# A second, word-by-word load of layer 3's adjacency in place of its transposition on TensorE

## The chip, the cores and the metric

The kernel runs on one core of one Trainium2 chip. The metric is device time in microseconds, the time of that core from the first to the last instruction of one execution. Before the change three runs took 2528.9, 2530.66 and 2531.29 us; the median, 2530.66 us, is the time that the change is compared with.

A core has engines that run beside each other, each through its own list of instructions in a fixed order: PE (TensorE, matrix products and transpositions), DVE (VectorE), ACT (ScalarE), POOL (GpSimd) and SP (SyncE, used here for starting transfers alone). Transfers (DMA) are carried out by 16 DMA engines; an instruction on SP or on ACT starts one.

## The reference, cut to what matters

128 graphs of 64 nodes with 256 features each pass four layers. `adj` holds a 64x64 matrix of zeros and ones for each graph, in fp32; the inputs make it symmetric, but the kernel doesn't count on that.

```python
# layers 0 and 1: masked / weighted attention with 8 heads, layer 2: five GRU steps on the graph
# (most of the work), each with a layer norm and a relu ahead and a residual sum after.
# layer 3:
def _L3_gnn_ref(x, adj, theta, W_h, W_t, b_t):
    in_degrees = jnp.sum(jnp.abs(adj), axis=-1)
    norm = ((in_degrees + 1e-06) ** (-0.5))[..., None]
    f_hom = jnp.einsum('bnd,de->bne', x, theta) * norm
    f_hom = jnp.einsum('bnm,bmd->bnd', adj, f_hom) * norm      # <- needs adj turned, see below
    f_het = jnp.einsum('bnd,de->bne', x, W_h)
    gate = jax.nn.sigmoid(jnp.einsum('bnd,de->bne', x, W_t) + b_t)
    out = gate * f_hom + (1.0 - gate) * f_het
    return jax.nn.elu(out)
```

TensorE contracts over partitions, and its stationary operand stands with the contracted index on the partitions. For `adj @ f_hom` the contracted index is m, so the kernel needs adj with m on the partitions: adj turned. A load in the natural order has n there.

## The kernel before

Graphs go two by two: a pair fills the 128 partitions (two graphs of 64 nodes), and four pairs make a group, so there are 16 groups. Each group g passes a **front** (layers 0 and 1 and the preparation of what layers 2 and 3 need), an **entry** and five **GRU steps** (layer 2), and a **back** (layer 3). The fronts, steps and backs of neighbouring groups are interleaved: while group g is in its GRU steps, the front of a later one and the back of an earlier one fill the gaps.

The order of instructions on each engine is set when the program is built, by a list scheduler (`Plan`). Every operation is added with an engine, a guessed cost, a guessed latency to its users, what it reads and writes, and a **due time** (its key, in units of a group). The scheduler then steps through time: of the operations that are ready on an engine, it takes the one that is due first, but none that is due more than `AHEAD` later than the oldest one that still waits. Constants shift and stretch the due times of the parts:

```python
AFTER = {"PE": 210, "DVE": 125, "ACT": 145, "POOL": 90, "SP": 2500}   # guessed latencies, ns
GROUP = 157000                                                        # ns of a group, for due times
BESIDE, ALONE, TURNING, AHEAD = 0.45, 0.15, 0.25, 2.15
FRONT, FRONT_LAST, FRONT_SPAN = 0.1, 0.2, 0.95
BACK, BACK_LAST, BACK_SPAN = -0.1, 0.35, 0.65
...
# in Plan.run: users' due times are handed back to what they need
for op in reversed(self.ops):
    for u in op.users:
        op.key = min(op.key, u.key - (op.cost + self.delay(op, u)) / GROUP)
```

The values and buffers: `new(tag, shape, n)` takes one of n buffers of that name; `bank` is one of four PSUM banks shared by nearly everything that isn't a gate of the GRU. The part of the front that the change touches:

```python
def load_adj(i):                       # two groups' adjacency, natural order, on SP
    t = new("adjq", [P, n_adj, NODES], 2, f"adjq{i}")
    dma(256, lambda: nc.sync.dma_start(t.tile, adj_t[:, i * n_adj : (i + 1) * n_adj, :]), [], [t])

blk = filled("adjblk", [P, PAIRS, P], 0.0)          # once: zeros, 128 x (4 pairs x 128)

def front(g):
    adjq = adj_vals[g // ADJ_GROUPS][0]
    neg = ...                                        # mask for layer 0, from adjq
    for layer in range(2):
        for half in range(2):
            attend(layer, xt, half, ...)
    for gp in range(2):                              # the two graphs of a pair, on the diagonal
        s = slice(gp * NODES, (gp + 1) * NODES)
        pool(350, lambda s=s: nc.gpsimd.tensor_copy(blk[s, :, s], adjq[s, sel, :]), [adjq], [(blk, gp)])
    A = ...                                          # adj != 0, for layer 2 (DVE)
    deg = ...; norm = ...                            # sums over rows (DVE), power (POOL)
    adjT = new("adjT", [P, PAIRS, P], 4, f"adjT_{g}")
    ps = bank(f"adjT_{g}")
    def turn():                                      # 4 transpositions of 128 x 128
        for p in range(PAIRS):
            nc.tensor.transpose(ps[:, p * P : (p + 1) * P], blk[:, p, :], ident.tile)
    pe(437, turn, [blk, ident], [ps], holds=[adjT], mode=TURN)
    for p in range(PAIRS):                           # out of PSUM, times the norm of column m
        sca(act(P, 1), lambda p=p: nc.scalar.activation(
            adjT[:, p, :], ps[:, p * P : (p + 1) * P], AF.Identity, scale=norm[:, p : p + 1]),
            [ps, norm], [(adjT, p)])
    held[g] = xt, A, adjT, norm
```

`adjT` is used once, in the back, some 3.6 groups later (group 4: transposed at 422 us, used from 972 us):

```python
pe(mm(256), lambda p=p, f=f, ph=ph: nc.tensor.matmul(
    ph[:, :D], adjT[:, p, :], f(), start=True, stop=True), [adjT, (v, 0), (v, 1)], [ph], holds=[o])
```

Transfers are started by SP, but for one short block at the start, in which ACT starts six small ones (`fill_rows`: the rows of biases and the node mask). During the GRU steps SP loads 1344 KB of fused gate weights for each step (`gv`, two buffers) and, for the attention, seven blocks of 192 KB (`qw`, seven buffers).

Of the kernel before, what the change touches and what calls it, by code (L numbers as in the profile page):

```python
# [10 lines left out]
AF = mybir.ActivationFunctionType  # L11
# [12 lines left out]
P = 128  # L24
D = 256
NODES = 64
HEADS = 8
HD = 32
PAIRS = 4
# [20 lines left out]

WIDE, T64, T32, TURN = range(4)
CHANGE = ((0, 95, 95, 0), (250, 30, 135, 200), (237, 135, 30, 187), (0, 95, 95, 0))
BESIDE = 0.45
ALONE = 0.15
TURNING = 0.25
AHEAD = 2.15

FRONT = 0.1  # L60
FRONT_LAST = 0.2
FRONT_SPAN = 0.95
BACK = -0.1
BACK_LAST = 0.35
BACK_SPAN = 0.65
STEP = 0.0
STEP_LAST = -0.1
STEP_SPAN = 0.5
LOCK = 0.3
BACK_END = 0.1  # L70
ENTRY = -0.05
FIRST = -1.2
FIRST_SPAN = 1.15
ORDER = (0, 0, 1, 0, 1, 0)
FUSE = -1.1
FUSE_SPAN = 0.25
# [53 lines left out]
class Plan:  # L130
# [63 lines left out]
    def shift(last, mode, small):  # L194

        if mode in (T64, T32):
            return -BESIDE if last in (T64, T32) else ALONE if small < 2 else 0.0
        return -TURNING if mode == TURN and last in (T64, T32) else 0.0

    def run(self):  # L200
# [12 lines left out]
        for _ in range(len(self.ops)):  # L213
            while due[0] in done:
                due.pop(0)
            best, horizon = None, due[0].key + AHEAD
            for eng, ops in ready.items():
# [54 lines left out]
def gnn_stack_kernel(ctx: ExitStack, tc: tile.TileContext, a: dict, out: bass.AP):  # L272
    nc = tc.nc
    x, adj, nodemask = a["x"], a["adj"], a["nodemask"]
    n_pairs = x.shape[0] // 2
    n_groups = n_pairs // PAIRS
    scale = 1.0 / math.sqrt(HD)

    x_t = x.rearrange("(t a) n d -> (a n) t d", a=2)
    out_t = out.rearrange("(t a) n d -> (a n) t d", a=2)  # L280
    adj_t = adj.rearrange("(t a) n k -> (a n) t k", a=2)

    work = ctx.enter_context(tc.tile_pool(name="work", bufs=1))
    dram = ctx.enter_context(tc.tile_pool(name="dram", bufs=1, space=bass.MemoryType.DRAM))
# [3 lines left out]
    plan = Plan()  # L288
    tags = {}

    def new(tag, shape, n, name=None):
        if tag not in tags:
            home = psum if tag in ("a", "g") else dram if tag in ("gates", "kept") else work
            tags[tag] = Slots(home, tag, n, tag in ("g", "ht", "agg", "Ta", "Th", "gv", "qw", "hTQ", "qk", "kexp", "v"))
        return Val(tags[tag], name or tag, shape)

    def bank(name):
        return new("a", [P, 512], 4, name)
# [4 lines left out]
    def pe(cost, fn, reads, writes, early=0.0, holds=(), mode=WIDE, leaves=None):  # L303
        plan.add("PE", cost, fn, reads, writes, early=early, holds=holds, mode=mode, leaves=leaves)

    def vec(cost, fn, reads, writes, early=0.0):
        plan.add("DVE", cost, fn, reads, writes, early=early)

    def vec2(cost, fn, reads, writes, early=0.0):

        plan.add("DVE", cost, fn, reads, writes, early=early, port=True)
# [4 lines left out]
    def pool(cost, fn, reads, writes, early=0.0, port=1):  # L316
        plan.add("POOL", cost, fn, reads, writes, early=early, port=port)

    def dma(kb, fn, reads, writes, n=1):
        plan.add("SP", max(450 * n, 60 + kb * 5), fn, reads, writes)  # L320
# [6 lines left out]
    def load_adj(i):  # L327
        t = new("adjq", [P, n_adj, NODES], 2, f"adjq{i}")
        dma(256, lambda: nc.sync.dma_start(t.tile, adj_t[:, i * n_adj : (i + 1) * n_adj, :]), [], [t])
        adj_vals[i] = [t, None]  # L330
# [16 lines left out]
    def filled(tag, shape, value, on_dve=False):  # L347
        t = new(tag, shape, 1)
        n = 1
        for s in shape[1:]:  # L350
            n *= s
        if on_dve:
            vec2(n * 0.55 + 75, lambda: nc.vector.memset(t.tile, value), [], [t])
        else:
            pool(n * 0.88 + 50, lambda: nc.gpsimd.memset(t.tile, value), [], [t])
        return t
# [13 lines left out]
    with plan.strand(-3.0, 0.1):  # L370
# [13 lines left out]
        ident = new("ident", [P, P], 1)  # L384
# [40 lines left out]
        for c, tag in enumerate(("ht", "agg")):  # L425
            t = new(tag, [P, 3 * D], 2 if tag == "ht" else 1, f"w_ih{c}")
# [45 lines left out]
    with plan.strand(-0.3, 0.1):  # L472

        b_rz = new("b_rz", [P, 4], 1)
        vec(160, lambda: nc.vector.tensor_add(b_rz.tile, cols[:, 4:8], cols[:, 10:14]), [cols], [b_rz])
        vec(160, lambda: nc.vector.tensor_scalar(b_rz.tile, b_rz.tile, 0.5, None, op0=ALU.mult),
            [b_rz], [b_rz])


        b_n = new("b_n", [P, 2], 1)  # L480
        vec(160, lambda: nc.vector.tensor_sub(b_n.tile, cols[:, 8:10], cols[:, 14:16]), [cols], [b_n])


        w3 = new("w3", [P, 3, 8, P], 1)

        def load_w3():
            for i, name in enumerate(("L3_gnn_theta", "L3_gnn_W_t", "L3_gnn_W_h")):
                nc.sync.dma_start(w3[:, i, :4, :].rearrange("p (c o) q -> p c (o q)", c=2),
                                  a[name].rearrange("(c p) o -> p c o", p=P))

        dma(768, load_w3, [], [w3], 3)
        b_t = load_row("L3_gnn_b_t")
        blk = filled("adjblk", [P, PAIRS, P], 0.0)


    def power(dst, src, at, eps, n, name):
# [649 lines left out]
    def front(g):  # L1146

        if g % ADJ_GROUPS == 0 and (g // ADJ_GROUPS + 1) * ADJ_GROUPS < n_groups:
            load_adj(g // ADJ_GROUPS + 1)
        xt = x_vals.pop(g)  # L1150
        adjq = adj_vals[g // ADJ_GROUPS][0]
        sel = slice((g % ADJ_GROUPS) * PAIRS, (g % ADJ_GROUPS + 1) * PAIRS)
        first = (g % ADJ_GROUPS) * PAIRS
        neg = new("neg", [P, PAIRS, NODES], 1, f"neg_{g}")
        vec2(200, lambda: nc.vector.tensor_scalar(
            neg.tile, adjq[:, sel, :], 0.0, NEG, op0=ALU.is_le, op1=ALU.mult), [adjq], [neg])
        for layer in range(2):
            if layer and not g % ADJ_GROUPS:
                log_adj(g // ADJ_GROUPS)
            ladj = adj_vals[g // ADJ_GROUPS][1]  # L1160
            for half in range(2):
                bias = ladj if layer else neg
                bias_at = (lambda p, t=ladj, n=first: t.tile.rearrange("p t k -> p (t k)")[:, (n + p) * NODES : (n + p + 2) * NODES]) if layer else (
                    lambda p, t=neg: t.tile.rearrange("p t k -> p (t k)")[:, p * NODES : (p + 2) * NODES])
                attend(layer, xt, half, bias, bias_at, f"{g}_{layer}_{half}", g < 2 - layer)
                if g and g + 1 < n_groups and layer and not half:
                    load_x(g + 1)
                yield
        flush(xt)
        for gp in range(2):  # L1170
            s = slice(gp * NODES, (gp + 1) * NODES)
            pool(350, lambda s=s: nc.gpsimd.tensor_copy(blk[s, :, s], adjq[s, sel, :]), [adjq], [(blk, gp)])

        A = new("A", [P, PAIRS, NODES], 3, f"A_{g}")
        vec2(250, lambda: nc.vector.tensor_scalar(A.tile, adjq[:, sel, :], 0.0, None, op0=ALU.not_equal),
             [adjq], [A])
        deg = new("deg", [P, PAIRS], 2, f"deg_{g}")
        vec(310, lambda: nc.vector.tensor_reduce(
            deg.tile, adjq[:, sel, :], axis=AX.X, op=ALU.add, apply_absolute_value=True), [adjq], [deg])
        norm = new("norm", [P, PAIRS], 5, f"norm_{g}")  # L1180
        power(norm, deg, lambda: deg.tile, 1e-6, PAIRS, f"deg_{g}")
        adjT = new("adjT", [P, PAIRS, P], 4, f"adjT_{g}")
        ps = bank(f"adjT_{g}")

        def turn():
            for p in range(PAIRS):
                nc.tensor.transpose(ps[:, p * P : (p + 1) * P], blk[:, p, :], ident.tile)

        pe(437, turn, [blk, ident], [ps], holds=[adjT], mode=TURN)

        for p in range(PAIRS):
            sca(act(P, 1), lambda p=p: nc.scalar.activation(
                adjT[:, p, :], ps[:, p * P : (p + 1) * P], AF.Identity, scale=norm[:, p : p + 1]),
                [ps, norm], [(adjT, p)])
        held[g] = xt, A, adjT, norm

    def entry(g, xt):
# [147 lines left out]
    parts = {g: front(g) for g in range(n_groups)}  # L1345
    with plan.strand(FIRST, FIRST_SPAN):
        for g in ORDER:
# [18 lines left out]
    for at, g, l in events:  # L1366
        last = g + 1 == n_groups
        if l < 0:
            with plan.strand(begin[g] - 1 + FRONT + (FRONT_LAST if last else 0), FRONT_SPAN):
                for _ in range(4 - taken[g]):  # L1370
# [7 lines left out]
        if l == 0:  # L1378
            xt, A, adjT, norm = held[g]
            with plan.strand(begin[g] + ENTRY, 0.1):  # L1380
                h, ht = entry(g, xt)
            held[g] = xt, h, adjT, norm
            chains[g] = gru(h, ht, A, str(g), last)
        with plan.strand(at + STEP + (STEP_LAST if last else 0), STEP_SPAN):
            next(chains[g])
        if l + 1 == LAYERS:
            with plan.strand(begin[g] + 2 + BACK + (BACK_LAST if g + 2 == n_groups else BACK_END if last else 0), BACK_SPAN):
                back(g, *held.pop(g))
# [34 lines left out]
```

## Time and profile before

| what | before |
|---|---|
| median of three runs | 2530.66 us |
| span of the profiled run | 2527.0 us |
| PE busy | 2498.2 us (99%) |
| DVE busy | 2031.1 us (80%) |
| ACT busy | 1394.3 us (55%) |
| POOL busy | 879.0 us (35%) |
| the main queue's packets, share of 16 DMA engines | 21.8% |
| chain that ended last, share of PE | 96% |

The page gives each engine's busy time as a share of the span, then the span in 40 slices with one digit of busy tenths each. The chain that ended last is followed back from the last instruction: at each step to what released it, or to the instruction before it on its engine. A list of groups shows, for each line and operation, the number of instructions, their busy time, the mean of one, and the idle time of the engine before them with what ended it. TensorE's work is pipelined: neighbouring records overlap, so the time that an operation takes from TensorE is read from the starts of neighbouring instructions and not from one record's duration. "PEld" is the loading of the stationary operand, which overlaps the products. An engine's name with a q (SPq, ACTq) stands for its queue: there the instructions that start transfers are shown, which don't count as busy.

### The profile page before, as it was taken

The numbers are of one execution on the slowest core, as the hardware profiler recorded it, in microseconds if no ns is written. First come the engines' busy times: TensorE is split into PE (matmuls) and PEld (weight loads), VectorE is DVE, ScalarE is ACT, GpSimd is POOL, SyncE is SP. The second block draws the span as 40 slices with busy tenths as digits, with TensorE's granted clock in tenths as the row PEclk, the third lists the DMA queues.
The fourth block names the chain that finished last, engine by engine and source line by source line (L and its number), as shares of the span: only waits on it lengthen the run. The fifth ranks groups of instructions, "written<-read, shape, count | busy, mean of one in ns | idle before, by whom it ended". The sixth has DMA issues, their size and how long they took to land.

```text
span 2527.0 us, 58120 instructions
## 1 busy us (share of the span) xinstructions
PE 2498.2 (99%) x23491; PEld 2147.7 (85%) x23491; DVE 2031.1 (80%) x4632; ACT 1394.3 (55%) x2806; POOL 879.0 (35%) x892
## 2 busy tenths in 40 slices
PE   8999999999999999999999999999999999999998
PEld 6788888888888888888888888888888888888885
DVE  6876788887878888788877978878788887878667
ACT  4456555555555555565555655556555555655454
POOL 5533323324333233333323333243332333333221
PEclk9999999999999999999999999999999999999999
DMA  5421222113121122221222121131311222211120
GB/s 181 168 85 64 72 70 79 54 62 105 49 96 67 45 93 71 79 71 65 66 68 101 50 83 56 61 101 49 101 64 50 82 71 79 71 49 67 49 71 18
DMA packets 78256, 188.47 MB, mean 75 GB/s; under 512 B 14802, under 2 KB 66852, under 8 KB 67108
## 3 DMA queue, kind: packets, MB, share of 16 engines
q1 hardware_dynamic: 77872, 184.71, 21.8%
q8 instruction: 186, 3.05, 0.5%
q14 instruction: 82, 0.67, 0.1%
q10 hardware_dynamic: 116, 0.04, 0.0%
HBM read 166.70 MB, written 18.02 MB: 73 GB/s over the span
## 4 chain that ended last, share of the span: by engine, by line
PE 96%; DVE 3%; ACT 1%; DMA 0%; issue 0%; POOL 0%; SPq 0%; DVEq 0%; ACTq 0%; POOLq 0%
PE gb L924 22%; PE gc L924 17%; PE nb L924 11%; PE nc L924 8%; PE qkvb L674 6%; PE qkvc L674 5%; PE y L810 4%; PE agg L964 3%; PE l3b L1246 3%; PE s L736 3%; PE l3c L1246 2%; PE lnT L514 2%; PE hT L514 2%; PE aT L778 2%; PE o L797 2%; PE hom L1313 1%
## 5 line engine op out<-in xcount | busy, mean ns | idle before, releaser
L1033 POOL TENSOR_TENSOR sn<-h,sn 128x512 f32<-128x512 f32 x158 | 208.8, 1325 | 449.4 <-ACT sn L1031 449.1
L500 POOL TENSOR_TENSOR rstd<-pw,few 128x2 f32<-128x2 f32 x128 | 102.1, 798 | 478.1 <-DVE pw L499 461.3
L772 POOL TENSOR_TENSOR e<-e,ssum 128x512 f32<-128x512 f32 x128 | 149.9, 1178 | 312.3 <-DVE ssum L771 284.7
L924 PE MATMUL gb<-Th,w_hh 128*128 128x256 f32 x960 | 248.3, 381 | 0.0
L924 PE MATMUL gb<-Ta,gv 128*128 128x256 f32 x960 | 246.4, 379 | 0.0
L893 POOL TENSOR_TENSOR Th<-h 128x256 f32<-128x256 f32 x160 | 129.0, 826 | 270.0 <-PE nb L924 190.6
L924 PEld LDWEIGHTS gb<-Th,w_hh 128*128 128x128 f32 x960 | 178.0, 190 | 28.7 <-POOL Th L893 0.4
L924 PEld LDWEIGHTS gb<-Ta,gv 128*128 128x128 f32 x960 | 180.0, 190 | 25.5
L1031 ACT ACTIVATE sn<-sn,b_n 128x512 f32<-128x512 f32 x158 | 114.2, 724 | 129.7 <-DVE sn L1029 128.2
L924 PE MATMUL gc<-h,w_hh 128*128 128x256 f32 x640 | 165.9, 382 | 0.1
L924 PE MATMUL gc<-agg,gv 128*128 128x256 f32 x640 | 165.5, 381 | 0.0
L1035 DVE SCALAR_TENSOR_TENSOR sn<-sg,sn 128x512 f32<-128x512 f32 x158 | 107.3, 686 | 54.8 <-POOL sn L1033 54.3
L1016 ACT ACTIVATE sg<-sg,b_rz 128x512 f32<-128x512 f32 x158 | 105.6, 715 | 79.6 <-DVE sg L996 79.6
L924 PE MATMUL nb<-Th,w_hh 128*128 128x256 f32 x480 | 144.3, 382 | 0.0
L924 PE MATMUL nb<-Ta,gv 128*128 128x256 f32 x480 | 143.0, 380 | 0.0
L893 POOL TENSOR_TENSOR Th<-h,Th 128x256 f32<-128x256 f32 x160 | 137.9, 862 | 10.2 <-DVE h L1037 4.5
L810 PE MATMUL y<-w_L_gnn_Wo,oT 128*128 128x256 f32 x512 | 138.6, 382 | 1.5 <-DVE oT L805 1.4
L1027 DVE SCALAR_TENSOR_TENSOR sn<-sg,sn 128x512 f32<-128x512 f32 x158 | 110.2, 699 | 32.9 <-ACT sn L1138 29.1
L924 PEld LDWEIGHTS gc<-agg,gv 128*128 128x128 f32 x640 | 118.7, 190 | 17.1 <-issue 2.5
L977 DVE TENSOR_TENSOR Ta<-agg 128x256 f32<-128x256 f32 x160 | 90.2, 577 | 52.3 <-PE nb L924 40.7
L924 PEld LDWEIGHTS gc<-h,w_hh 128*128 128x128 f32 x640 | 116.6, 190 | 15.8 <-ACT sg L1023 0.5
L988 ACT ACTIVATE p5g<-gc 128x512 f32<-128x512 f32 x79 | 46.9, 593 | 149.4 <-PE gc L924 149.4
(223 smaller groups left out, 6931.9 us busy)
## 6 DMA issues: line engine op xcount, KB each, us to landing
gv<-gates SPq DMA_DIRECT2D x80, 1344.0 KB, 6.0
qw<-kept SPq DMA_DIRECT2D x203, 192.0 KB, 2.5
x<-in_x_dram SPq DMA_DIRECT2D x32, 256.0 KB, 5.6
out_dram<-x SPq DMA_DIRECT2D x32, 256.0 KB, 2.3
gates<-gv SPq DMA_DIRECT2D x5, 1344.0 KB, 4.7
adjq<-in_adj_dram SPq DMA_DIRECT2D x8, 256.0 KB, 3.0
gw<-in_L_gnn_weight_dram SPq DMA_DIRECT2D x5, 256.0 KB, 5.2
kept<-s SPq DMA_DIRECT2D x8, 128.0 KB
```

What stands on the lines that cost most here:

```text
L500: pool(660 if n == 2 else 970, lambda: nc.gpsimd.tensor_tensor(dst.tile, s.tile, few[:, 1 : 1 + n], op=ALU.pow), [s, (few, 1)], [dst], port=2)
L674: nc.tensor.matmul(bk[:, j * P : (j + 1) * P], lhs, rhs, start=first and j == 0, stop=True, skip_group_check=True)
L772: pool(1000, lambda e8=e8, z=z: nc.gpsimd.tensor_tensor(e8(), e8(), z[:, :, None].to_broadcast(shape), op=ALU.mult), [e, z], [e])
L810: pe(mm(256), lambda i=i, c=c: nc.tensor.matmul(py[:, i * D : (i + 1) * D], oT[:, i, c, :], w_o[:, c, :], start=c == 0, stop=c == 1), [(oT ...
L893: pool(690, lambda: nc.gpsimd.tensor_tensor(T[:, i, :], x(), y(), op=ALU.subtract), reads, [(T, i)])
L924: nc.tensor.matmul(bank_[:, col * HALF : (col + 1) * HALF], at(g, n), rhs(), start=first and j == 0, stop=True, skip_group_check=True)
L1016: sca(act(TOK, 1.5), lambda k=k, col=col: nc.scalar.activation(g_v[:, :, k, :], g_v[:, :, k, :], AF.Tanh, bias=b_rz[:, col : col + 1], sca ...
L1027: vec2(dve(TOK), lambda: nc.vector.scalar_tensor_tensor(a_(), r(), 1.0, a_(), op0=ALU.add, op1=ALU.mult), [*ts[0], n_v], [n_v])
L1031: sca(act(TOK, 1.5), lambda: nc.scalar.activation(a_(), a_(), AF.Tanh, bias=b_n[:, oc : oc + 1]), [n_v, b_n], [n_v])
L1033: pool(1230, lambda: nc.gpsimd.tensor_tensor(b_(), hh(), a_(), op=ALU.subtract), [*hp, n_v], [n_v])
L1035: vec2(dve(TOK), lambda: nc.vector.scalar_tensor_tensor(b_(), z(), 1.0, b_(), op0=ALU.add, op1=ALU.mult), [*ts[1], n_v], [n_v])
L1246: pe(mm(384), lambda: nc.tensor.matmul(bk[:, : 3 * P], b(), w3[:, :, n, :], start=first, stop=True, skip_group_check=True), [w3, *reads], ...
```

## The change: a load turned by the access pattern

The adjacency is in DRAM already, so it can be read a second time in another order. The new view has the contracted index k on the partitions:

```diff
     adj_t = adj.rearrange("(t a) n k -> (a n) t k", a=2)
+    adj_turned = adj.rearrange("(t a) n k -> a k t n", a=2)
```

On partition k it steps through n, and two neighbouring n lie 64 words apart in DRAM: each word of four bytes is a piece of its own. The front of each group starts eight such transfers from ACT's queue (2 graphs of a pair x 4 pairs, 64 x 64 words each) into the diagonal blocks of `adjT`, which POOL clears first. ACT then multiplies by the norm in place, from SBUF and no longer out of PSUM.

```diff
 def front(g):
     ...
+        adjT = new("adjT", [P, PAIRS, P], 4, f"adjT_{g}")
+        pool(620, lambda: nc.gpsimd.memset(adjT.tile, 0.0), [], [adjT])
+
+        def load_turned():
+            for gp in range(2):
+                s = slice(gp * NODES, (gp + 1) * NODES)
+                for p in range(PAIRS):
+                    nc.scalar.dma_start(adjT[s, p, s], adj_turned[gp, :, g * PAIRS + p, :])
+
+        plan.add("ACT", 1000, load_turned, [], [adjT], lat=30000)
     ... (mask, attention of layers 0 and 1)
-        for gp in range(2):
-            s = slice(gp * NODES, (gp + 1) * NODES)
-            pool(350, lambda s=s: nc.gpsimd.tensor_copy(blk[s, :, s], adjq[s, sel, :]), [adjq], [(blk, gp)])
     ... (A, deg, norm)
-        adjT = new("adjT", [P, PAIRS, P], 4, f"adjT_{g}")
-        ps = bank(f"adjT_{g}")
-
-        def turn():
-            for p in range(PAIRS):
-                nc.tensor.transpose(ps[:, p * P : (p + 1) * P], blk[:, p, :], ident.tile)
-
-        pe(437, turn, [blk, ident], [ps], holds=[adjT], mode=TURN)
 
         for p in range(PAIRS):
             sca(act(P, 1), lambda p=p: nc.scalar.activation(
-                adjT[:, p, :], ps[:, p * P : (p + 1) * P], AF.Identity, scale=norm[:, p : p + 1]),
-                [ps, norm], [(adjT, p)])
+                adjT[:, p, :], adjT[:, p, :], AF.Copy, scale=norm[:, p : p + 1]),
+                [adjT, norm], [(adjT, p)])
```

The buffer of zeros, `adjblk`, goes, with its one memset. For the scheduler, the eight starts are one operation of ACT with a cost of 1000 ns, whose result is there 30000 ns later.

The due times are set anew with it, so the order of instructions on every engine changes somewhat:

```diff
-BESIDE = 0.45            +BESIDE = 0.25
-AHEAD = 2.15             +AHEAD = 2.1
-FRONT_LAST = 0.2         +FRONT_LAST = 0.15
-BACK_SPAN = 0.65         +BACK_SPAN = 0.6
-STEP_LAST = -0.1         +STEP_LAST = -0.15
-BACK_END = 0.1           +BACK_END = 0.05
-ENTRY = -0.05            +ENTRY = 0.15
-FIRST = -1.2             +FIRST = -1.4
-FIRST_SPAN = 1.15        +FIRST_SPAN = 1.55
```

The change is for TensorE: it takes the transpositions of the adjacency, their PSUM bank and POOL's copies out of the program, and gives the turning to the DMA engines.

More of the change, by code (lines that the diff above doesn't have):

```diff
@@ L52 @@
 CHANGE = ((0, 95, 95, 0), (250, 30, 135, 200), (237, 135, 30, 187), (0, 95, 95, 0))
-BESIDE = 0.45
+BESIDE = 0.25
 ALONE = 0.15
 TURNING = 0.25
-AHEAD = 2.15
+AHEAD = 2.1
 FRONT = 0.1
-FRONT_LAST = 0.2
+FRONT_LAST = 0.15
 FRONT_SPAN = 0.95
@@ L64 @@
 BACK_LAST = 0.35
-BACK_SPAN = 0.65
+BACK_SPAN = 0.6
 STEP = 0.0
-STEP_LAST = -0.1
+STEP_LAST = -0.15
 STEP_SPAN = 0.5
 LOCK = 0.3
[L70 to L73, printed above, removed]
+BACK_END = 0.05
+ENTRY = 0.15
+FIRST = -1.4
+FIRST_SPAN = 1.55
 ORDER = (0, 0, 1, 0, 1, 0)
@@ L492, in gnn_stack_kernel @@
         b_t = load_row("L3_gnn_b_t")
-        blk = filled("adjblk", [P, PAIRS, P], 0.0)
     def power(dst, src, at, eps, n, name):
```

## The prediction, made before the changed kernel was run

> **What bounds the kernel now.** I read the page's busy shares first, then the chain that ended last, and then the waits of TensorE.
>
> ```profile
> PE 2498.2 (99%) x23491; PEld 2147.7 (85%) x23491; DVE 2031.1 (80%) x4632; ACT 1394.3 (55%) x2806; POOL 879.0 (35%) x892
> ...
> PE 96%; DVE 3%; ACT 1%; DMA 0%; issue 0%; POOL 0%; SPq 0%; DVEq 0%; ACTq 0%; POOLq 0%
> ```
>
> PE is busy for 2498.2 of 2527.0 us, and 96% of the chain is PE. A busy share alone can mislead, so I asked who PE waits for, and for the busy time of the steady part (158 to 2212 us):
>
> ```profile
> PE pc L449 <- DMA w_v<-in_L_gnn_Wv_dram: 8.9, 1, 8.9
> PE y L810 <- DVE oT L805: 1.4, 1, 1.4
> PE f L1217 <- ACT hT L519: 1.4, 2, 1.1
> PE gb L924 <- ACT agg L970: 1.2, 2, 0.9
> ...
> 158.00:2212.00 2054.00, 2052.02 (x19675) 1782.95 (x19674) 1677.40 (x3855) 1160.04 (x2359) 710.89 (x704) 1.00 0.22 71
> ```
>
> The columns of the waits are total, times and longest in us. One wait of 8.9 us stands at the start, for the first data; no other is above 1.4 us in total. In the second view the first pair is length and PE busy: in 2054 us PE lacks 2 us. So the kernel is bound by PE's instruction stream: whatever leaves PE comes off the time, and whatever makes PE wait is added in full, as PE has no idle time in which to catch up.
>
> Now the part that the change removes. This is the view of the tile adjT, and one stretch of PE's timeline:
>
> ```profile
> L1187 PE MATMUL adjT<-ident,adjblk x64: 272/273/329, 36.5 to 2107.8; 128*128 128x128 f32 x64
> L1172 POOL COPY adjblk<-adjq x32: 391/487/631, 31.3 to 2011.3; 64x256 f32<-64x256 f32 x32
> L1192 ACT ACTIVATE adjT<-adjT,norm x64: 359/378/410, 50.4 to 2109.1; 128x128 f32<-128x128 f32 x64
> ...
> 1187.91 0.60 PE L1187 MATMUL adjT<-ident,adjblk 128*128 128x128 f32 x4
> 1188.35 1.03 PE L924 MATMUL gc<-Th,w_hh 128*128 128x256 f32 x4
> ```
>
> One record lasts 273 ns, but the four of a group start at 1187.91 and the next product at 1188.35: four transpositions take 0.44 us from PE, 0.11 us each.
>
> **What the Trainium skill says.** TensorE: Matmul & The Clock Gate, section Part 4: PE-mode transpose, gives some 275 ns for a 128x128 transposition in a kernel, in bf16. This trace's fp32 records agree (273 ns), but what one takes away in a stream is 0.11 us; the measured spacing decides. DMA: Bandwidth & Descriptors, section Rules for kernel authors, says that a strided last dimension is lowered to one descriptor for each element, and that a transposition by rearranged access pattern is 19 times slower than the chip's own DMA transposition. The kernel before has no such transfer, so its trace can't confirm that. The section Issuing engines are not separate DMA queues of that page says that transfers started from ACT and from SP run on the same 16 DMA engines and interleave. So ACT's queue brings no bandwidth of its own.
>
> **The change part by part.**
>
> *Off PE.* 16 groups x 0.44 us = **7.0 us**. This is on the path in full. The PSUM bank that it held is worth nothing visible, as PE waits for no bank.
>
> *POOL.* It loses 32 copies x 487 ns = 15.6 us and one memset; it gains 16 memsets of 128x512, for which the memset of adjblk has a duration (542 ns): 8.7 us. POOL is busy 35%: no effect.
>
> *ACT's 64 multiplications* stay (378 ns each, now from SBUF). No effect.
>
> *The DMA engines.* A group's eight transfers carry 8 x 4096 words; by the skill one descriptor each, so over 16 engines 2048 for each engine and group. What does a word cost? Two stretches give the time of a packet: between 1514 and 1516 us the adjacency is loaded in 1024 packets of 256 B, and from 10 to 15 us weights in packets of 1024 B.
>
> ```profile
> 1514.00:1515.00 1.00, 1.00 (x7) 0.87 (x6) 0.32 (x1) 0.89 (x2) 0.65 (x1) 1.00 0.90 207
> 1515.00:1516.00 1.00, 1.00 (x6) 0.90 (x5) 0.97 (x2) 0.19 (x1) 0.00 (x0) 1.00 0.25 55
> ...
> 10.00:15.00 5.00, 4.31 (x13) 3.47 (x13) 1.79 (x8) 0.60 (x1) 0.70 (x1) 1.00 1.07 357
> ```
>
> The last two columns are DMA share and GB/s. (0.90 + 0.25) us x 16 / 1024 = 18 ns for 256 B; 1.07 x 5 us x 16 / (1785 KB / 1 KB = 1743) = 49 ns for 1024 B. The straight line through both meets 4 B at about 8 ns. My estimate is 8 to 15 ns a word; the kernel's own guess (30 us for 2048) is the upper end. So a group's turned load keeps all 16 engines occupied for **16 to 30 us out of 153**, and the DMA share rises from 22% to 32 to 42%. In steady state this is hidden: the turned adjacency is needed 3.6 groups later (group 4: transposed at 422 us, used from 972 us), and the gate weights (6.0 us to land) have a whole GRU step, some 30 us, between the release of a buffer and its next use. Slowed twofold for 30 us they are still in time, mostly.
>
> *The start.* There it is not hidden so well. Up to 25 us the DMA share is about 1 (1.07 above, 1.09 from 20 to 25 us), and PE's first weights come in that stretch. adjT has four buffers and ACT is idle early, so the first turned loads go out in the first tens of us and share the engines with those weights. I expect a delay of **3 to 12 us**, of which I take 6.
>
> *Starting eight transfers on ACT.* This is the dear part. At the start of the kernel before, ACT starts the rows and the mask; this is its queue:
>
> ```profile
> 1.34 0.24 ACTq L395 DMA_DIRECT2D rows<-in_L_gnn_bk_dram  x1
> 1.61 0.27 ACTq L395 DMA_DIRECT2D rows<-in_L_gnn_b_ih_dram  x1
> 1.92 0.32 ACTq L395 DMA_DIRECT2D rows<-in_L_gnn_b_hh_dram  x1
> ...
> 3.51 0.60 ACTq L397 DMA_DIRECT2D rows<-in_nodemask_dram  x1
> ```
>
> A start takes 0.24 to 0.60 us, say 0.38: eight take 3.0 us in one piece, against 1.0 us in the plan. ACT's order is fixed, so all behind it comes up to 2 us late. Does PE feel it? One case: the second agg copy leaves ACT at 662.33 us and PE's product with it starts at 663.10, 0.8 us of slack. ACT stands idle for 45% of the span, but in short pieces: in the steady part I count 24 idle stretches of at least 2.6 us, under two for each group. I take half of the 2 us as lost, with a spread of 0 to 1.5 us for a group: 16 x 0.6 = **10 us**, from my choice of 0.6.
>
> Sum: -7.0 + 6 + 10 = +9 us. The new due times can take back some of it; such a retuning is worth a few us at most where PE already has 2 us of idle time in 2054. I take -3, so about +6: **2537 us**.
>
> **The rivals.**
>
> *A: PE's gain comes through whole.* If starts on ACT fall into its idle time and the startup keeps its pace, -7 us and perhaps a little more from the due times: 2518 to 2524 us. For it speaks that PE hardly ever waits in the kernel before, although the plan's costs are guesses: its slack absorbs errors of some tenths of a us. Against it speaks that 3 us isn't some tenths.
>
> *B: ACT is held at the starts.* If a start can't be handed over until the transfers ahead of it have made room, ACT stands for most of the 16 to 30 us of each group, and PE with it: 16 x 5 to 20 us, or 2600 to 2850 us. The queue of SP speaks for it a little: behind the large stores at the start, four starts together took 6.95 us and a single one of x 1.59 us:
>
> ```profile
> 71.66 6.95 SPq L565 DMA_DIRECT2D kept<-s  x4
> 78.65 1.59 SPq L343 DMA_DIRECT2D x<-in_x_dram  x1
> ```
>
> (the first with waits for data in it). Against it: behind loads alone, with 1 MB and more outstanding in the first 17 us, SP's starts kept to 0.37 to 0.65 us. But no transfer there had 256 pieces for each engine. I give a clear form of this a little over one in five.
>
> *C: the weights come late.* The words and the gate weights share the engines, and a gv or qw load that lands after its turn stops PE for some us in each group: 2540 to 2600 us. Against it: the slack above, some 30 us against a burst of 16 to 30.
>
> **Range and chances.** A alone gives the low end, 2516 with a little from the due times. My sum stands at 2537. B and C make the tail above; I put the high end at 2620. Two per cent are 50.6 us: faster by that much would need seven times what leaves PE, 0.01; slower, above 2581 us, is B or a strong C, 0.22; the rest, 0.77, is within.
>
> **What would show it.** (1) PE has 64 instructions less, and its busy time falls by 7 us. (2) The queue of ACT shows 128 starts: at 0.3 to 0.4 us each my lumps are right; at 1 us or more it is B. (3) The waits of PE show new entries with ACT as releaser, 0.3 to 1.5 us each, some 10 us in sum; if there are none, A. (4) PE busy in the first 160 us (146.9 before) is some us lower. (5) The DMA share in the steady part is 0.32 to 0.42; gv takes more than 6.0 us to land in the median of its slow loads, but no PE wait names gv or qw; if one does, C. The prediction fails if ACT's starts block it, or if the time of a word is far above 15 ns.

## The result and the profile after

The changed kernel takes **2864.18 us** in the median (four runs, 2863.6 to 2865.23) against 2529.96 us for the kernel before on the same chips: 1.132 times the time, 95% interval 1.130 to 1.134. The prediction was 2537 us with a range of 2516 to 2620 us. It was wrong, and by far.

The page of the changed kernel, the parts that answer to those shown of the kernel before (busy times, DMA queues, the chain that ended last):

```profile
PE 2534.1 (89%) x23427; PEld 2158.6 (75%) x23427; DVE 2030.9 (71%) x4632; ACT 1411.8 (49%) x2806; POOL 839.8 (29%) x875
...
q1 hardware_dynamic: 77872, 184.71, 19.5%
q10 hardware_dynamic: 526452, 2.15, 10.5%
...
PE 71%; ACTq 8%; DVE 5%; POOL 2%; issue 2%; ACT 1%; POOLq 0%; DVEq 0%
PE gb L924 18%; PE gc L924 12%; PE nb L924 9%; ACTq L1162 8%; PE nc L924 6%; PE qkvb L674 5%; PE qkvc L674 3%; PE y L810 3%; PE agg L964 2%; PE l3b L1246 2%; PE hT L514 2%; PE l3c L1246 2%; PE lnT L514 2%; PE aT L778 2%; PE o L797 1%
```

The chain points to the place: PE's share falls from 96% to 71%, and 8% of the span is `ACTq L1162`, the line that starts the turned loads. PE has its 64 instructions less. It is idle for 2861.8 - 2534.1 = 328 us, against 29 us before.

The waits of PE (total, times, longest in us), and the tile adjT (durations in ns, least/median/most):

```profile
PE nb L924 <- DVE sg L996: 203.1, 12, 17.5
PE q L629 <- ACT hT L519: 49.8, 1, 49.8
PE aT L778 <- POOL e L772: 21.3, 2, 20.5
...
L1162 ACTq DMA_DIRECT2D adjT<-in_adj_dram x128: 602/2354/5930, 5.1 to 2421.6; - x128
L1313 PE MATMUL hom<-F,adjT x128: 379/379/483, 442.0 to 2854.1; 128*128 128x256 f32 x128
```

A start on ACT takes 2.35 us in the median, where the prediction took 0.38. PE now has a pause of 17 us in each of 12 groups and one of 50 us at the start. The waits don't name ACT in the groups, and here one has to look further: PE waits for DVE's `sg`, but that stood behind something itself. This is one group in order of time, ACT first, then DVE, then PE:

```profile
1011.85 17.88 ACTq L1162 DMA_DIRECT2D adjT<-in_adj_dram  x8
1029.77 0.72 ACT L1332 ACTIVATE F<-F 128x256 f32<-128x256 f32 x2 [17.98 <-DMA adjT<-in_adj_dram]
...
1030.22 0.42 DVE L1334 SCALAR_TENSOR_TENSOR o<-o,F 128x256 f32<-128x256 f32 x1 [16.61 <-ACT F L1332]
1032.50 0.68 DVE L996 TENSOR_TENSOR sg<-gc,ug 128x512 f32<-128x512 f32 x1
...
1015.67 1.03 PE L810 MATMUL y<-w_L_gnn_Wo,oT 128*128 128x256 f32 x4
1033.23 1.22 PE L924 MATMUL nb<-h,w_hh 128*128 128x256 f32 x2 [16.54 <-DVE sg L996]
1034.25 1.91 PE L924 MATMUL gb<-Th,w_hh 128*128 128x256 f32 x4
1035.95 1.78 PE L924 MATMUL gb<-h,w_hh 128*128 128x256 f32 x4
```

From 1011.85 to 1029.73 us ACT does nothing but start eight transfers. DVE, whose order is fixed as well, soon waits 16.6 us for ACT's Exp on F, and its sg, for which PE's next product waits, stands behind that. PE stops some 5 us after ACT and begins again 3.5 us after it. The products that follow are slow as well: four products take 1.7 us from one start to the next, where 0.86 is usual. The same stretch in windows (length, busy of PE, PEld, DVE, ACT, POOL, then TensorE's granted clock, DMA share, GB/s):

```profile
1015.00:1020.00 5.00, 1.70 (x8) 1.14 (x6) 0.00 (x0) 0.00 (x0) 0.00 (x0) 1.00 0.95 7
1020.00:1025.00 5.00, 0.00 (x0) 0.00 (x0) 0.00 (x0) 0.00 (x0) 0.00 (x0) 0.54 0.94 7
1025.00:1030.00 5.00, 0.00 (x0) 0.00 (x0) 0.00 (x0) 0.23 (x1) 0.00 (x0) 0.50 0.89 6
1030.00:1035.00 5.00, 1.77 (x4) 1.49 (x5) 4.78 (x11) 1.83 (x4) 0.00 (x0) 0.50 0.69 59
1035.00:1040.00 5.00, 5.00 (x19) 4.07 (x18) 3.95 (x8) 1.53 (x3) 1.27 (x1) 0.75 0.38 105
1040.00:1045.00 5.00, 5.00 (x83) 4.26 (x82) 4.78 (x14) 3.90 (x9) 1.67 (x2) 1.00 0.00 0
```

While ACT is held, the DMA engines are 90 to 95% busy and move 6 to 7 GB/s: words of four bytes. And the clock granted to PE falls to a half during the pause and stays there for some us after it.

The 335 us by which the span grew come from two parts. This is the product that uses adjT in the kernel before:

```profile
L1313 PE MATMUL hom<-F,adjT x128: 379/379/483, 363.7 to 2519.3; 128*128 128x256 f32 x128
```

adjT is first used at 442.0 us in place of 363.7: **78 us at the start**. From then on the first use in one group and in the next lie (2183.0 - 442.0) / 10 = 174.1 us apart (groups 0 to 10), before (1891.7 - 512.5) / 9 = 153.2 (groups 1 to 10; the first interval is shorter there, 148.8 us): **20.9 us for each of 12 groups, 251 us**. Together 329; most of the rest is that first interval. At the start the queue of ACT shows this, sixteen starts in a row with the first activation behind them (it begins at 58.7 us, before at 10.2):

```profile
5.06 52.27 ACTq L1162 DMA_DIRECT2D adjT<-in_adj_dram  x16
57.36 1.28 ACT L519 ACT_TABLE_LOAD   x1 [57.36 <-DMA r_L_gnn_bo<-in_L_gnn_bo_dram]
```

### The profile page after: what moved, and what is told of

The parts are those of the page before. It is cut to its first block, busy times and chain, and to the rows that moved or that the text cites. A ratio compares the mean times of both kernels' runs of the same rounds, so it can differ in the third digit from the quotient of the medians.

```text
span 2861.8 us, 58190 instructions
## 1 busy us (share of the span) xinstructions
PE 2534.1 (89%) x23427; PEld 2158.6 (75%) x23427; DVE 2030.9 (71%) x4632; ACT 1411.8 (49%) x2806; POOL 839.8 (29%) x875
## 3 DMA queue, kind: packets, MB, share of 16 engines
q10 hardware_dynamic: 526452, 2.15, 10.5%
## 4 chain that ended last, share of the span: by engine, by line
PE 71%; ACTq 8%; DVE 5%; POOL 2%; issue 2%; ACT 1%; POOLq 0%; DVEq 0%
PE gb L924 18%; PE gc L924 12%; PE nb L924 9%; ACTq L1162 8%; PE nc L924 6%; PE qkvb L674 5%; PE qkvc L674 3%; PE y L810 3%; PE agg L964 2%; PE l3b L1246 2%; PE hT L514 2%; PE l3c L1246 2%; PE lnT L514 2%; PE aT L778 2%; PE o L797 1%
## 5 line engine op out<-in xcount | busy, mean ns | idle before, releaser
L924 PE MATMUL gb<-Th,w_hh 128*128 128x256 f32 x960 | 259.8, 395 | 10.6 <-POOL sn L1033 10.6
L924 PE MATMUL nb<-h,w_hh 128*128 128x256 f32 x160 | 55.4, 431 | 203.1 <-DVE sg L996 203.1
L772 POOL TENSOR_TENSOR e<-e,ssum 128x512 f32<-128x512 f32 x128 | 139.3, 1099 | 285.7 <-DVE ssum L771 140.9
L924 PEld LDWEIGHTS nb<-h,w_hh 128*128 128x128 f32 x160 | 29.7, 208 | 214.4 <-DVE sg L996 212.0
L1334 DVE SCALAR_TENSOR_TENSOR o<-o,F 128x256 f32<-128x256 f32 x64 | 26.7, 417 | 207.3 <-ACT F L1332 207.0
L1035 DVE SCALAR_TENSOR_TENSOR sn<-sg,sn 128x512 f32<-128x512 f32 x158 | 107.0, 683 | 77.8 <-POOL sn L1033 77.4
L1332 ACT ACTIVATE F<-F 128x256 f32<-128x256 f32 x64 | 25.2, 412 | 256.7 <-DMA adjT<-in_adj_dram 202.1
L893 POOL TENSOR_TENSOR Th<-h,Th 128x256 f32<-128x256 f32 x160 | 128.3, 802 | 7.6 <-DVE h L1037 4.5
```

Of the source, the lines that this page charges most:

```text
L772: pool(1000, lambda e8=e8, z=z: nc.gpsimd.tensor_tensor(e8(), e8(), z[:, :, None].to_broadcast(shape), op=ALU.mult), [e, z], [e])
L893: pool(690, lambda: nc.gpsimd.tensor_tensor(T[:, i, :], x(), y(), op=ALU.subtract), reads, [(T, i)])
L924: nc.tensor.matmul(bank_[:, col * HALF : (col + 1) * HALF], at(g, n), rhs(), start=first and j == 0, stop=True, skip_group_check=True)
L1035: vec2(dve(TOK), lambda: nc.vector.scalar_tensor_tensor(b_(), z(), 1.0, b_(), op0=ALU.add, op1=ALU.mult), [*ts[1], n_v], [n_v])
```

## The experiments

Theory 1 was that ACT is held at its starts because the words ahead of them have yet to be drained (rival B of the prediction). Its rivals were the number of starts, the load on the DMA engines as such, and the new due times. Unless it is said, an experiment has the new due times and is told against the changed kernel.

### The same eight starts with rows in place of words

```diff
-    adj_turned = adj.rearrange("(t a) n k -> a k t n", a=2)
+    adj_turned = adj.rearrange("(t a) n k -> a n t k", a=2)
```

The turning is left out. As adj is symmetric in these inputs, the sums stay the same.

> The same eight starts for each group on ACT, at the same places, but in natural order: 64 rows of 256 B in place of 4096 words each (the turning is left out; adj is symmetric in these inputs, so the sums are the same). Theory 1 (ACT is held because the words queue up): a start takes 0.3 to 0.6 us, eight 2.5 to 4 us; time 2525 to 2545 us. Rival (any eight starts in one piece on ACT, or the new due times, cost the time): 2780 us or more.

Measured: 2643.13 us, 1.045 times before (1.043 to 1.046). It lies between the two forecasts and meets neither. The tile adjT and one group:

```profile
L1162 ACTq DMA_DIRECT2D adjT<-in_adj_dram x128: 472/607/1805, 5.4 to 2201.2; - x128
...
903.27 5.00 ACTq L1162 DMA_DIRECT2D adjT<-in_adj_dram  x8
908.32 0.72 ACT L1332 ACTIVATE F<-F 128x256 f32<-128x256 f32 x2 [5.10 <-DMA adjT<-in_adj_dram]
911.78 0.75 PE L924 MATMUL nb<-h,w_hh 128*128 128x256 f32 x2 [3.59 <-DVE sg L996]
...
PE nb L924 <- DVE sg L996: 52.5, 12, 4.9
```

With rows a start takes 0.61 us in the median and ACT is held for 5 to 6 us, not for 18; so the words account for 221 of the 334 us. But eight starts in one piece cost 113 us even so: a group is 161.4 us long, 8.2 us more than before. A piece of 5 us on ACT stops PE for 3.6 us here (52.5 us in 12 such waits, 4.4 us each), and a slower clock follows it.

### Half of the words

```diff
-  nc.scalar.dma_start(adjT[s, p, s], adj_turned[gp, :, g * PAIRS + p, :])
+  nc.scalar.dma_start(adjT[s, p, s.start : s.start + 32], adj_turned[gp, :, g * PAIRS + p, :32])
```

Half of the turned adjacency is left out.

> The eight starts carry 32 columns each, half of the words (2048, 128 for each DMA engine); half of the turned adjacency is left out. Theory 1: ACT is held about half as long, 8 to 10 us a group in place of 18; time 2660 to 2720 us. If the limit is a number of words that may wait, two or three starts at the head of each eight are short (0.4 to 0.7 us); if it is one transfer at a time, the second already takes about 1.2 us. Rival (the number of starts counts): 2850 us.

Measured: 2751.67 us, a single run. Nearly halfway between rows and words, and above what theory 1 gave; that forecast did not have in it what eight starts in one piece cost even with rows, 113 us.

```profile
L1162 ACTq DMA_DIRECT2D adjT<-in_adj_dram x128: 602/1358/4257, 5.2 to 2311.0; - x128
961.51 10.37 ACTq L1162 DMA_DIRECT2D adjT<-in_adj_dram  x8
```

ACT is held for 10.4 us in that group. In the later groups, the first start of each eight takes 0.60 us and the second already 1.2 us or more (602 and 1209 ns in this group); with all words it is 0.60 and then 2.1 to 3.6 us. A packet of one word takes 9.1 ns: 10.5% of 2861.8 us on 16 engines, over 526452 packets. So 128 words for each engine are 1.2 us and 256 are 2.3 us, about what a start takes when another stands ahead of it. From ACT one such transfer is drained, it seems, before the next is handed over.

The times from start to landing, where the traces have them, fit this: in the median 2.1 us with rows, 4.4 with half of the words and 6.6 with all. What comes on top of the rows is about two drains, 2 x 1.2 and 2 x 2.3 us, one for the transfer ahead and one for the transfer itself. It also shows that the start isn't held until the transfer ahead has landed. Whether it is held until the last word has moved or only until the last word has been handed to the DMA engines, these runs don't separate.

### Eight starts apart from each other, on ACT

```diff
-        plan.add("ACT", 1000, load_turned, [], [adjT], lat=30000)
+        for i in range(2 * PAIRS):         # each at least 3.5 us after the one before
+            gp, p = i % 2, i // 2
+            s = slice(gp * NODES, (gp + 1) * NODES)
+            plan.add("ACT", 600, lambda s=s, gp=gp, p=p: nc.scalar.dma_start(
+                adjT[s, p, s], adj_turned[gp, :, g * PAIRS + p, :]),
+                [(adjT, ("w", i - 1))] if i else [], [(adjT, ("w", i))],
+                lat=3500 if i < 2 * PAIRS - 1 else 8000)
```

> All words, all eight starts on ACT, but as eight operations of their own that the scheduler puts at least 3.5 us apart, each planned with 0.6 us. Theory 1: each start then finds the one ahead of it drained (2.3 us) and takes 0.6 us; ACT is held 5 us a group in eight small pieces, PE loses 0 to 0.5 us for each; time 2525 to 2590 us. Rival (the words disturb by their load on the DMA engines, wherever their starts stand): 2780 us or more.

Measured: 2568.35 us, 1.016 (1.014 to 1.017). The same words on the same queue of the same engine, and 296 us of the 334 are gone:

```profile
L1161 ACTq DMA_DIRECT2D adjT<-in_adj_dram x128: 602/603/7181, 5.5 to 2153.1; - x128
L1313 PE MATMUL hom<-F,adjT x128: 379/379/483, 390.2 to 2552.9; 128*128 128x256 f32 x128
```

The median of a start is 0.60 us, as forecast, and a group is 153.5 us long, 0.3 more than before. From 539 to 2072 us PE is busy for 1532.97 of 1533 us, at a DMA share of 0.35. This rules out the load on the DMA engines as the main cause. What is left is the start of the kernel: adjT is first used at 390.2 us, 26 us later than before and 36 us later than in the run with the due times alone (below), which is the closer comparison; 38 us of time are left to explain. Starts there take up to 7.2 us, while the weights come (DMA share 1.00 in the first 160 us).

### The same on SP

`nc.sync` in place of `nc.scalar`, and "SP" in place of "ACT" in the plan.

> The same eight spaced starts on SP, which does nothing but start transfers. Theory 1: no compute engine is held; gate weights can come 2 to 5 us late, within their slack of some 30 us; time 2518 to 2540 us, near the 7 us that left PE. Rival (the words make gv and qw late): PE waits for gv or qw by several us a group, 2600 us or more.

Measured: 2548.44 us, 1.007 (1.006 to 1.009); above the forecast, far below the rival. The start is as fast as before (first use at 358.3 us); SP starts the first turned load at 18.6 us, behind those of weights, where ACT started it at 5.1. But a group takes 154.9 us, 1.7 us more than before and 1.2 more than with the due times alone (153.7). The waits of PE show most of that:

```profile
PE gb L924 <- POOL sn L1033: 9.7, 11, 0.9
...
PE qkvb L674 <- DMA qw<-kept: 3.1, 1, 3.1
```

The wait of 0.9 us for POOL's `sn` comes in 11 groups and not once in the run with the due times alone. Why `sn` comes late here is open.

### The due times alone

The kernel before with the nine new constants.

> The kernel before with the nine new due times alone; the transpositions on TensorE stay. Theory 1 (ACT held by the turned loads is the cost): the due times are a matter of a few us, 2520 to 2550 us. Rival (the due times, fitted to the plan and not to the chip, are a main part): 2580 us or more.

Measured: 2530.55 us, 0.9999 (0.999 to 1.0008). The due times neither cost nor bring anything that can be measured here.

```profile
L1313 PE MATMUL hom<-F,adjT x128: 379/379/483, 354.3 to 2517.3; 128*128 128x256 f32 x128
```

They do move its parts: adjT is first used 9 us sooner than before, and a group takes 153.7 us, 0.5 more. Set against this run, which has the changed kernel's due times and the turning of before, the start of the changed kernel costs 88 us and not 78, and a group 20.4 us and not 20.9.

### No turning at all: the bound of the gain

The due times of before; the second load is out, and POOL copies the natural blocks to adjT:

```diff
-  (memset of adjblk, copies to adjblk, four transpositions, activation out of PSUM)
+  pool(620, lambda: nc.gpsimd.memset(adjT.tile, 0.0), [], [adjT])
+  pool(350, lambda s=s: nc.gpsimd.tensor_copy(adjT[s, :, s], adjq[s, sel, :]), [adjq], [(adjT, ("b", gp))])
+  (activation in place, as in the changed kernel)
```

> Bound of the gain: no second load and no transposition, POOL copies the natural blocks straight into adjT, due times of before (the turning is left out; adj is symmetric in these inputs). What leaves PE is 16 x 0.44 us = 7.0 us: 2520 to 2526 us. Rival (the transpositions filled gaps that other work doesn't): 2528 us or more.

Measured: 2527.5 us, 0.999 (0.998 to 0.9999), between the two. Of 7.0 us, 2.4 arrive. A group is 153.4 us long, not 152.8 (153.2 less 0.44): with 0.44 us less to do, the scheduler finds another order, and in it other seams open. In eight groups there are 64 places before where PE goes from wide products to small ones (agg, s and o, in tiles of 64 or 32 rows), and 72 here. Such a seam takes 0.3 us from one start to the next, where 0.22 is usual between wide products, and the way back 0.17 us, where small products follow each other in 0.02. By these figures, 8 more seams with their ways back make about 0.2 us a group (an estimate); the rest of the 0.6 us is open.

### Spaced starts with the due times of before, on ACT and on SP

> The turned load in eight spaced starts on ACT, with the due times of before. If the new due times cost the 38 us that the spaced starts with the new times stood above before: about 2530 us. If it is the start of the kernel, where the words share the DMA engines and hold ACT while the weights come: 2545 to 2570 us, with PE some 25 us short of before in the first 160 us.

> The turned load in eight spaced starts on SP, with the due times of before. If the due times are to blame for the slower groups (154.9 us in place of 153.2), the group falls to about 152.7 us and the time to 2520 to 2528 us, faster than both kernels. If SP's held queue is (gate and attention weights some us late), the group stays at about 155 us and the time at 2540 to 2555 us.

Measured: 2586.53 us on ACT (1.023, 1.021 to 1.025), above the range given, and 2550.08 us on SP (1.008, 1.007 to 1.010). Neither becomes faster than the kernel before. In both a group takes 154.8 us in the median. As it is the same on ACT and on SP, a held SP is hardly the reason here. In both there are 88 seams in eight groups, 24 more than before, by the figures above some 0.7 us a group, and in both PE waits 0.6 us for DVE's oT in 11 groups:

```profile
PE l3c L1246 <- DVE oT L805: 6.4, 11, 0.6
```

That is the line of the run on SP; on ACT it is 6.3 us. Both speak for the order of the instructions, which wasn't tried by itself. Of the 2.0 us that a group takes above 152.8, about 0.7 stay open. On ACT the start is again late (first use at 397.0 us; PE is busy for 115.5 of the first 160 us, 31 us less than before).

### The first four groups on SP, the others on ACT

```diff
+  plan.add("SP" if g < 4 else "ACT", 600, lambda ..., q=nc.sync if g < 4 else nc.scalar: q.dma_start(...))
```

> Eight spaced starts for each group, new due times: on SP for the first four groups, whose words go out while the kernel starts, on ACT for the other twelve. If the 38 us of the spaced starts on ACT are the start of the kernel (first use of adjT at 390 us in place of 364) and not the later groups (153.4 us each there), both losses are avoided: 2530 to 2540 us. If the spaced starts on ACT cost something in every group that the first four hide, 2550 us or more.

Measured: 2534.23 us, 1.0014 (1.0007 to 1.0021), within the first forecast. First use at 360.9 us, 153.5 us for a group; with the due times alone it was 354.3 and 153.7. So the loss of the spaced starts on ACT was that of the kernel's start. The turned load is now all but hidden, and gains nothing.

### Spaced starts on POOL

`nc.gpsimd`, "POOL" and 1200 ns in the plan.

> The eight spaced starts on POOL, new due times, each planned with 1.2 us. POOL is busy a third of the time. If POOL is free after about a us (the words queue elsewhere): 2525 to 2550 us. If it is held per word as ACT is (2 us or more for each of the 4096-word transfers), its sums and differences for the GRU come late: 2570 to 2750 us, with PE's waits naming POOL.

Measured: 2611.81 us, 1.032 (1.031 to 1.034), with POOL in PE's waits, as the second forecast had it.

```profile
L1161 POOL DMA_DIRECT2D adjT<-in_adj_dram x128: 1615/1642/1803, 3.1 to 2206.8; - x128
...
PE aT L778 <- POOL e L772: 24.6, 8, 9.4
PE gb L924 <- POOL sn L1033: 10.6, 12, 0.9
...
PE gc L924 <- POOL Th L893: 8.9, 12, 0.7
```

But the reason given for it doesn't hold as it stood: a start takes 1.64 us in the median, 1.80 at most, and doesn't grow when others stand ahead. It is a fixed piece of work, 210 us in all, on an engine whose results the GRU waits for. The waits for `e` all lie in the first 140 us, those for `sn` are the same in the changed kernel, and those for `Th` are new. Set against the due times alone, adjT is first used 42 us later (396.6 us) and a group takes 157.0 us, 3.3 more. The main queue's packets also take more of the DMA engines here, 26.0% in place of 21.8% before; what part of the loss is POOL's time and what part slower transfers was not separated.

## Why the prediction was wrong

**Off PE, 7.0 us: the instructions went, the time mostly didn't.** The bound measured 2.4 us. PE's busy time in the changed kernel didn't fall by 7 but rose by 36 us, as its clock was lower (0.956 of full in the mean, 0.999 before).

**The DMA engines: right.** The estimate was 8 to 15 ns a word, the trace has 9.1; one packet for each word, 4096 and 16 more for each transfer, so the first claim quoted from the Trainium skill holds; the 19 times no run here shows. The DMA share of a group is 0.29 to 0.31, just under the forecast of 0.32 to 0.42, as the groups are longer; with the starts spaced on ACT it is 0.35. Gate weights land in 5.8 us, before 6.0, and no wait of PE names gv or qw: rival C, weights that come late, is out for the changed kernel.

**Starting eight transfers on ACT: the step that failed.** It had 0.38 us for a start, eight in 3.0 us, and a loss of 0.6 us a group. Each of the three terms was wrong. The start by itself takes 0.6 us (rows). Behind another turned transfer it takes the 2.3 us in which that one's words are drained, so ACT is held for 18 us. And PE doesn't lose 0.6 us of 2 us of excess but nearly all of it: 16.9 us of pause in a group for 18 us on ACT, 4.4 us for 5 to 6. (The prediction calls its 0.6 half of the 2 us; half is 1.0, or 16 us in all, which would have changed little.) The 0.38 came from the transfers of biases and mask at the start of the kernel before, of 1 to 32 KB in pieces of 512 B; nothing there had words as pieces, and the prediction named this gap and still gave it one in five.

The Trainium skill, DMA: Bandwidth & Descriptors, section Issuing engines are not separate DMA queues, adds to what the prediction took from it that starting on several engines only saves the sequencer's time, which is "usually small relative to the DMA itself". This is a case outside that "usually": in this trace the engine is held for 17.9 us by eight transfers that keep the DMA engines busy for 8 x 2.3 = 18.4 us: of all the transfers only the last runs beside the engine's work.

**The start: a term was missing.** 3 to 12 us were forecast from shared bandwidth. With the first words on SP, adjT is first used 4 to 7 us later than with the due times alone, so that term, if it is bandwidth, was of the right size. But in the changed kernel it was 88 us (78 against the kernel before), with ACT held 52 us ahead of its first activation and PE busy for 79.8 of the first 160 us (146.9 before); with the words spaced on ACT it was still 36.

**Rival B** was the right mechanism (ACT stands for most of 16 to 30 us: 18), and its range of 2600 to 2850 us ended just short: it had 5 to 20 us for a group and nothing more for the start or the clock. The evidence used against it, that SP's starts behind loads alone stayed at 0.37 to 0.65 us, was of transfers with at most 64 pieces for each DMA engine.

**The clock** was in no step. The Trainium skill, TensorE: Matmul & The Clock Gate, section Why this matters for your kernels, warns of idle gaps of more than some 3 us between products. The trace agrees: in the kernel before no pause after the start is longer than 1.4 us and the clock stays at 1.00 until the last stretch; here a pause of 16.5 us is followed by half speed until 1037.5 us, which costs about 2 us more. Pause (16.9), a wait for POOL's sn (0.9) and half speed (2) make 19.8 of the 20.9 us of a group; the rest wasn't followed up.

## What to carry to other kernels

ACT, when it also computes, shouldn't start transfers made of single words back to back: here each start waited until the words of the one ahead had been drained (256 words for each DMA engine: 2.3 us), and as ACT's order is fixed, that time was lost to all that stood behind. If it must be, put the starts further apart than one transfer takes, or on an engine that does nothing else; spacing them, with the first ones on SP, took 1.132 times the time before to 1.001. And where the bound engine has no idle time, removing a fraction of a per cent of its work may bring less than that: of 7.0 us, 2.4 arrived here, as the order of the rest moved too.

## What the runs showed of the hardware beyond expectation

- A transfer of 64 x 64 single words takes 0.60 us to start with nothing ahead of it, and about 2.3 us behind another; with half of the words 1.2 to 1.7 us for most; with rows of 256 B 0.5 to 0.6 us for nearly all. From start to landing it is 6.6, 4.4 and 2.1 us.
- Started from POOL, the same transfer holds the engine 1.64 us at any time, and its words don't show as one packet each: 10240 packets in 128 transfers, 80 for each, against 4112 from ACT.
- A pause of 3.6 us on PE is enough for a stretch at a lower clock: in the run with rows the granted clock was 0.89 over the 15 us from 905 to 920 us.
